# A quarter of the weight product moved from the front of a graph kernel into the first graph's chain

## The chip, the cores and the metric

The kernel runs on one core of a Trainium2 chip. The metric is the device time of one execution in microseconds (us). A kernel's time is the median over its runs. The profile is one profiled execution; its span is 1.7 to 1.9 us shorter than the device time of the same kind of run.

A ratio of two kernels is the mean time of one kernel's fast runs over the mean of the other's fast runs of the same rounds. It is therefore not quite the ratio of the medians that are quoted.

## The reference, cut to what matters

64 graphs, each with 256 nodes and 512 features, go through two layers. Layer 0 aggregates neighbours and multiplies by weights; layer 1 scores each node and weights its value by a softmax over the 256 nodes.

```python
# layer 0
deg = sum(adj, -1);  agg = adj @ x / max(deg, EPS)
x = layernorm(x + relu(concat([x, agg]) @ W.T))
# layer 1
q, k = split(x @ Wqk);  v = x @ Wv
w = inv_scale * mask * sum(q * (adj @ (k * mask)), -1)
x = layernorm(x + softmax(w, axis=nodes) * v)
```

The kernel uses that q·(adj·k) needs only the product of the two halves of Wqk, which it computes once at the front, as four chunks of 128 rows. Products of 2x2 blocks use seven multiplications in place of eight, so there are sums of blocks (the tiles s, sa, tv, t) to be made by VectorE and GpSimd.

## The kernel before: the parts that matter

The front multiplies the weights, then the graphs are pipelined: graph i's layer 0, graph i-1's aggregation for layer 1 together with graph i's, and graph i-2's layer 1.

```python
ps = [ps_mm.tile([P, F], F32, name="mm") for _ in range(NF)]          # four banks
for a in range(NA):
    for c in range(NF):
        nc.tensor.matmul(ps[c], wqk[:, a, c * P:(c + 1) * P], wqk[:, NA + a, :],
                         start=(a == 0), stop=(a == NA - 1))
for c in range(NF):
    nc.scalar.copy(w1[:, c, :], ps[c])
...
def weight_sums(w, name):                 # four 1024-wide subtractions on VectorE
    ...
    nc.vector.tensor_sub(t1, b12, b11)
    nc.vector.tensor_sub(t2, b22, t1)
    nc.vector.tensor_sub(b12, b22, b12)
    nc.vector.tensor_sub(t4, b21, t2)     # the only one that reads chunk 3
...
def layer0_a(g):
    ...
    product(u, s["S3"], w["T3"], start=False)
    nc.scalar.copy(y[:, 1, :], u)                       # stall 1 waits for this copy
    nc.vector.tensor_add(y[:, 1, :], p5, y[:, 1, :])
def layer0_b(g):
    ...
    product(u, s["A22"], w["T4"], start=False)          # T4's product, in the same bank u
    nc.scalar.copy(own[:, 1, :], u)
    product(p5, s["S4"], w["B22"], start=False)
    nc.vector.tensor_add(y[:, 0, :], p5, y[:, 0, :])    # stall 2: the aggregation needs y
```

The scheduler may reorder what is not held; `tc.issue_after(x)` holds instructions of x's engine behind x.

## Time and profile before

| | kernel before |
|---|---|
| time, median (first 3 runs) | 1983.97 us (1983.8 to 1984.79) |
| span of the profile | 1982.8 us |
| TensorE busy | 1959.8 us, 99% |
| VectorE / ScalarE / GpSimd busy | 79% / 33% / 21% |
| first weights land | 5.07 us |
| layer 0 of graph 0 starts | 20.37 us |
| graph 1's T4 product starts | 48.83 us |
| last product starts, and lasts | 1970.47 us, 3.37 us |

TensorE has next to no idle time from graph 2 to the last graph, so whatever moves the pipeline's start moves its end by the same amount. That is why the last four rows cut the span into stretches. I call them:

- **F**: first weight-product record to the start of layer 0 (before: 20.37 - 5.07 = 15.30 us);
- **M**: start of layer 0 to graph 1's T4 product (48.83 - 20.37 = 28.46 us);
- **S**: from there to the start of the last product (1921.64 us);
- **L**: duration of the last product (3.37 us).

One fp32 matmul of 512 columns is two records of 0.429 us each.

### The profile page before, as it was taken

The numbers are of one execution on the slowest core, as the hardware profiler recorded it, in microseconds if no ns is written. First come the engines' busy times: TensorE is split into PE (matmuls) and PEld (weight loads), VectorE is DVE, ScalarE is ACT, GpSimd is POOL, SyncE is SP. The second block draws the span as 40 slices with busy tenths as digits, with TensorE's granted clock in tenths as the row PEclk, the third lists the DMA queues.
The fourth block names the chain that finished last, engine by engine and source line by source line (L and its number), as shares of the span: only waits on it lengthen the run. The fifth ranks groups of instructions, "written<-read, shape, count | busy, mean of one in ns | idle before, by whom it ended". The sixth has DMA issues, their size and how long they took to land.

```text
span 1982.8 us, 19678 instructions
## 1 busy us (share of the span) xinstructions
PE 1959.8 (99%) x5424; PEld 1018.5 (51%) x5424; DVE 1566.7 (79%) x3220; ACT 650.0 (33%) x1545; POOL 419.4 (21%) x518
## 2 busy tenths in 40 slices
PE   8999999999999999999999999999999999999997
PEld 3554555555555545555555555455555555554553
DVE  5677877888788778778887887787788878877877
ACT  2323333333233333333332333333333323333332
POOL 3122221221221222212112212222122122122200
PEclk9999999999999999999999999999999999999999
DMA  6333333333333333333333333333333333333311
GB/s 223 88 83 82 98 93 86 96 90 91 97 80 101 93 82 97 93 87 96 82 100 97 79 102 93 81 96 94 88 96 89 92 97 80 102 93 82 83 45 46
DMA packets 390493, 182.09 MB, mean 92 GB/s; under 512 B 281456, under 2 KB 355056, under 8 KB 390384
## 3 DMA queue, kind: packets, MB, share of 16 engines
q1 hardware_dynamic: 390384, 180.84, 33.9%
q8 instruction: 44, 0.72, 0.2%
q14 instruction: 65, 0.53, 0.1%
HBM read 114.10 MB, written 33.62 MB: 74 GB/s over the span
## 4 chain that ended last, share of the span: by engine, by line
PE 98%; DVE 1%; DMA 0%; ACT 0%; issue 0%; DVEq 0%
PE mm L162 77%; PE mm L262 19%; PE mm L131 1%; DMA wqk<-wqk_t 0%; DMA adj<-adj_t 0%; DVE st L185 0%; ACT vals L303 0%; DVE own L296 0%; ACT vals L225 0%; DVE o L396 0%; DVE vals L236 0%; DVE own L223 0%; DVE t L141 0%; DVE t L140 0%; DVE w L142 0%
## 5 line engine op out<-in xcount | busy, mean ns | idle before, releaser
L162 PE MATMUL mm<-w,s 128*128 128x512 f32 x1024 | 481.5, 592 | 1.4 <-ACT v L339 0.7
L162 PE MATMUL mm<-t,s 128*128 128x512 f32 x1024 | 462.1, 594 | 0.0
L162 PEld LDWEIGHTS mm<-t,s 128*128 128x128 f32 x1024 | 194.8, 190 | 243.6 <-issue 228.8
L162 PEld LDWEIGHTS mm<-w,s 128*128 128x128 f32 x1024 | 194.2, 190 | 193.4 <-issue 155.0
L162 PE MATMUL mm<-w,xT 128*128 128x512 f32 x512 | 240.9, 592 | 0.0
L162 PE MATMUL mm<-w,x1T 128*128 128x512 f32 x512 | 240.8, 592 | 0.0
L204 POOL TENSOR_TENSOR sa<-adj 128x128 f32<-128x128 f32 x64 | 45.9, 717 | 759.9 <-PE mm L262 758.4
L152 POOL TENSOR_TENSOR s<-xT 128x256 f32<-128x256 f32 x64 | 47.0, 734 | 706.5 <-PE mm L162 687.3
L262 PE MATMUL mm<-tv,sa 128*128 128x256 f32 x768 | 187.3, 379 | 0.4 <-DVE tv L252 0.4
L262 PEld LDWEIGHTS mm<-tv,sa 128*128 128x128 f32 x768 | 145.7, 190 | 75.8 <-issue 48.2
L236 DVE TENSOR_TENSOR vals<-mm,vals 128x512 f32<-128x512 f32 x64 | 44.2, 691 | 142.9 <-PE mm L162 142.9
L188 ACT ACTIVATE rstd<-mv,eps 128x2 f32<-128x2 f32 x129 | 38.0, 296 | 345.1 <-DVE mv L186 345.0
L162 PEld LDWEIGHTS mm<-w,xT 128*128 128x128 f32 x512 | 97.3, 190 | 94.7 <-issue 91.4
L162 PEld LDWEIGHTS mm<-w,x1T 128*128 128x128 f32 x512 | 97.1, 190 | 93.8 <-issue 90.4
L339 ACT COPY v<-mm 128x512 f32<-128x512 f32 x63 | 36.9, 586 | 283.2 <-PE mm L162 283.2
L162 PE MATMUL mm<-t,xT 128*128 128x512 f32 x256 | 126.7, 617 | 2.8 <-ACT vals L225 2.8
L162 PE MATMUL mm<-t,x1T 128*128 128x512 f32 x256 | 125.3, 612 | 0.0
L294 DVE SCALAR_TENSOR_TENSOR own<-zr,rdeg,own 128x512 f32<-128x512 f32 x128 | 107.6, 841 | 22.0 <-ACT zr L284 21.9
L262 PE MATMUL mm<-vals,adj 128*128 128x256 f32 x512 | 121.3, 379 | 1.9 <-DVE vals L236 1.9
L262 PEld LDWEIGHTS mm<-vals,adj 128*128 128x128 f32 x512 | 97.1, 190 | 43.6 <-issue 16.9
L218 ACT COPY own<-mm 128x512 f32<-128x512 f32 x64 | 37.5, 586 | 227.4 <-PE mm L162 227.4
L328 DVE SCALAR_TENSOR_TENSOR q<-mm,zr 128x512 f32<-128x512 f32 x126 | 84.7, 672 | 32.4 <-PE mm L162 32.4
(101 smaller groups left out, 2732.6 us busy)
## 6 DMA issues: line engine op xcount, KB each, us to landing
xT<-x_t SPq DMA_DIRECT2D x64, 512.0 KB
x<-x SPq DMA_DIRECT2D x64, 512.0 KB
x1T<-sq SPq DMA_DIRECT2D x1008, 32.0 KB
out<-o SPq DMA_DIRECT2D x63, 512.0 KB
adj<-adj_t SPq DMA_DIRECT2D x64, 256.0 KB
rows<-adj SPq DMA_DIRECT2D x64, 256.0 KB
row<-d SPq DMA_DIRECT2D x62, 128.0 KB
d<-turned SPq DMA_DIRECT2D x248, 0.2 KB
```

The costliest lines, as they stand in the source:

```text
L131: nc.tensor.matmul(ps[c], wqk[:, a, c * P:(c + 1) * P], wqk[:, NA + a, :], start=(a == 0), stop=(a == NA - 1))
L152: eng.tensor_add(s1, a21, a22)
L162: queued[0] = nc.tensor.matmul(ps, a[:, c, :], b[:, c, :], start=start and c == 0, stop=(c == H - 1), skip_group_check=True).ins
L188: nc.scalar.activation(rstd[:, :n], mv[:, :n, 1], AF.Ln, bias=eps)
L204: nc.gpsimd.tensor_add(sa[:, 0], a21, a22)
L218: began = nc.scalar.copy(own[:, 0, :], u)
L236: nc.vector.tensor_add(y[:, 0, :], p5, y[:, 0, :])
L262: nc.tensor.matmul(ps[:, k * HF:(k + 1) * HF], sumsA[g - k][a], w[b][:, n, :], start=start and n == 0, stop=True, skip_group_check=True)
L294: nc.vector.scalar_tensor_tensor(own[:, t, :], z[:, t, :], rdeg[:, t:t + 1], own[:, t, :], op0=OP.mult, op1=OP.add)
L328: nc.vector.scalar_tensor_tensor(q, a, 1.0, agg[:, t, :], op0=OP.mult, op1=OP.mult, accum_out=to)
L339: nc.scalar.copy(v[:, 0, :], u)
```

## The change

The intent: TensorE stalls in graph 0's chain, where nothing else is there to run. A quarter of the weight product (chunk 3, four matmuls) is taken out of the front and put into two of these stalls, half in each.

```diff
+    def weight_product(chunks, pause=NA):
+        ps = [ps_mm.tile([P, F], F32, name="mm") for _ in chunks]
         for a in range(NA):
-            for c in range(NF):
-                nc.tensor.matmul(ps[c], wqk[:, a, c * P:(c + 1) * P], wqk[:, NA + a, :],
+            for k, c in enumerate(chunks):
+                nc.tensor.matmul(ps[k], wqk[:, a, c * P:(c + 1) * P], wqk[:, NA + a, :],
                                  start=(a == 0), stop=(a == NA - 1))
-        for c in range(NF):
-            nc.scalar.copy(w1[:, c, :], ps[c])
+            if a + 1 == pause:
+                yield
+        for k, c in enumerate(chunks):
+            nc.scalar.copy(w1[:, c, :], ps[k])
+        yield
+    step(weight_product((0, 1, 2)), 2)
 ...
+    rest = weight_product((3,), NA // 2)
 ...
             began, added = layer0_a(i)
+        if i == 0:
+            step(rest)
 ...
             layer0_b(i)
+        if i == 0:
+            step(rest)
```

The rest of the diff keeps the weights' tile alive longer. The softmax of the last graph and its singly stored tiles, which the title of the change also names, stand in both kernels alike. What the diff does not show: the scheduler, seeing other times, also moves two of the four sums of layer 1's weights on VectorE, from before to after the subtractions that the aggregation needs.

More of the change, by code (lines that the diff above doesn't have):

```diff
@@ L100, in resnorm_kernel @@
     w1 = const.tile([P, 2 * NF, F], F32, name="w1")
-    setup = tc.tile_pool(name="setup", bufs=1)
-    with setup as sp:
-        wqk = sp.tile([P, 2 * NA, F], F32, name="wqk")
-        for a in range(NA):
-            src = wqk_t.rearrange("(h a p) f -> a p h f", p=P, h=2)[a]
-            first(wqk.rearrange("p (h a) f -> a p h f", h=2)[a], src)
-        w0_of = w_t.rearrange("(k h p) o -> k p h o", p=P, h=H)
-        for k in (0, 2):
-            first(w0[:, k * H:(k + 1) * H, :], w0_of[k])
-        load_t(0, first)
-        for k in (3, 1):
-            first(w0[:, k * H:(k + 1) * H, :], w0_of[k])
-        load(0, first)
-        mask_sb = const.tile([P, NT, B], F32, name="mask_sb")
-        first(mask_sb, mask_t)
-        load_t(1, first)
-        load(1, first)
-        loaded = first(w1[:, NF:, :], wv.rearrange("(c p) o -> p c o", p=P))
-        ident = const.tile([P, P], F32, name="ident")
-        make_identity(nc, ident)
-        eps = const.tile([P, 1], F32, name="eps")
-        nc.vector.memset(eps, LN_EPS)
-        wide = [const.tile([P, Q], F32, name=f"wide{k}") for k in (0, 1)]
-        for w in wide:
-            nc.vector.memset(w, 0.0)
-        ps = [ps_mm.tile([P, F], F32, name="mm") for _ in range(NF)]
-        for a in range(NA):
-            for c in range(NF):
-                nc.tensor.matmul(ps[c], wqk[:, a, c * P:(c + 1) * P], wqk[:, NA + a, :],
-                                 start=(a == 0), stop=(a == NA - 1))
-        for c in range(NF):
-            nc.scalar.copy(w1[:, c, :], ps[c])
@@ L135, in resnorm_kernel @@
-    late = ctx.enter_context(tc.tile_pool(name="late", bufs=2))
+    setup = ExitStack()
+    wqk = setup.enter_context(tc.tile_pool(name="setup", bufs=1)).tile([P, 2 * NA, F], F32, name="wqk")
+    for a in range(NA):
+        src = wqk_t.rearrange("(h a p) f -> a p h f", p=P, h=2)[a]
+        first(wqk.rearrange("p (h a) f -> a p h f", h=2)[a], src)
+    w0_of = w_t.rearrange("(k h p) o -> k p h o", p=P, h=H)
+    for k in (0, 2):
+        first(w0[:, k * H:(k + 1) * H, :], w0_of[k])
+    load_t(0, first)
@@ new lines, in resnorm_kernel @@
+    for k in (3, 1):
+        first(w0[:, k * H:(k + 1) * H, :], w0_of[k])
+    load(0, first)
+    mask_sb = const.tile([P, NT, B], F32, name="mask_sb")
+    first(mask_sb, mask_t)
+    load_t(1, first)
+    load(1, first)
+    loaded = first(w1[:, NF:, :], wv.rearrange("(c p) o -> p c o", p=P))
+    ident = const.tile([P, P], F32, name="ident")
+    make_identity(nc, ident)
+    eps = const.tile([P, 1], F32, name="eps")
+    nc.vector.memset(eps, LN_EPS)
+    wide = [const.tile([P, Q], F32, name=f"wide{k}") for k in (0, 1)]
@@ new lines, in resnorm_kernel @@
+    for w in wide:
+        nc.vector.memset(w, 0.0)
+    def weight_product(chunks, pause=NA):
+        ps = [ps_mm.tile([P, F], F32, name="mm") for _ in chunks]
+        for a in range(NA):
+            for k, c in enumerate(chunks):
+                nc.tensor.matmul(ps[k], wqk[:, a, c * P:(c + 1) * P], wqk[:, NA + a, :],
+                                 start=(a == 0), stop=(a == NA - 1))
+            if a + 1 == pause:
[3 more added lines that the diff above has]
+        yield
@@ L137, in weight_sums, with step @@
+    def step(gen, n=1):
+        for _ in range(n):
+            next(gen, None)
+    step(weight_product((0, 1, 2)), 2)
     def weight_sums(w, name):
@@ L464, in resnorm_kernel @@
     prepare(0)
-    def step(gen, n=1):
-        for _ in range(n):
-            next(gen, None)
+    rest = weight_product((3,), NA // 2)
     for i in range(B + LAG - 2):
@@ L474, in resnorm_kernel @@
         if i == 1:
+            setup.close()
+            late = ctx.enter_context(tc.tile_pool(name="late", bufs=2))
             W1 = weight_sums(w1, "t1_")
```

## The prediction

> **What bounds the kernel now.** I read the page first: part 1 for the engine that is full, part 4 for the chain that ends last.
>
> ```profile
> PE 1959.8 (99%) x5424; PEld 1018.5 (51%) x5424; DVE 1566.7 (79%) x3220; ACT 650.0 (33%) x1545; POOL 419.4 (21%) x518
> PE 98%; DVE 1%; DMA 0%; ACT 0%; issue 0%; DVEq 0%
> ```
>
> TensorE is busy for 1959.8 of 1982.8 us and makes up 98% of the chain. So only a shorter TensorE list or fewer TensorE gaps can shorten the run. The diff keeps all 5424 matmul records; only gaps can be won. The view of busy time by stretches says where gaps are: from 75 to 1940 us TensorE is busy in 1865.00 of 1865.00 us. The gaps lie before 75 us and after 1940 us. The second place is not touched: the last graph's softmax and its tiles stored singly, which the change's title names, are already in the kernel before, and a listing of both kernels' instructions by engine shows no difference there.
>
> The beginning, TensorE alone (start, duration, then what it is; in brackets the idle time ahead of it and who ended it):
>
> ```profile
> 5.07 15.46 PE L131 MATMUL mm<-wqk 128*128 128x512 f32 x32 [5.07 <-DMA wqk<-wqk_t]
> 20.37 1.88 PE L162 MATMUL mm<-w,xT 128*128 128x512 f32 x4
> ...
> 27.23 1.88 PE L162 MATMUL mm<-w,s 128*128 128x512 f32 x4
> 29.79 1.98 PE L162 MATMUL mm<-t,xT 128*128 128x512 f32 x4 [0.68 <-ACT vals L225]
> 31.61 1.88 PE L162 MATMUL mm<-w,s 128*128 128x512 f32 x4
> 34.64 1.13 PE L262 MATMUL mm<-vals,adj 128*128 128x256 f32 x4 [1.15 <-DVE vals L236]
> 36.20 0.67 PE L262 MATMUL mm<-tv,sa 128*128 128x256 f32 x2 [0.43 <-DVE tv L252]
> ...
> 48.83 1.98 PE L162 MATMUL mm<-t,xT 128*128 128x512 f32 x4 [1.65 <-ACT vals L225]
> ```
>
> The reader is to see that 32 records (16 fp32 matmuls, two records each) multiply the weights, then graph 0 runs alone and stalls three times, because each product accumulates in a bank that ScalarE or VectorE must read first. Graph 1 stalls once more at 48.83. Later stalls (0.79 us at 53.31, 0.51 us at 70.61) depend on the same chain.
>
> VectorE in the same stretch, which ends two of the stalls:
>
> ```profile
> 29.77 0.69 DVE L226 TENSOR_TENSOR vals<-mm,vals 128x512 f32<-128x512 f32 x1 [1.30 <-ACT vals L225]
> 30.38 1.22 DVE L140 TENSOR_TENSOR t<-w 128x1024 f32<-128x1024 f32 x1
> 31.63 1.23 DVE L141 TENSOR_TENSOR t<-w,t 128x1024 f32<-128x1024 f32 x1
> 32.77 1.22 DVE L142 TENSOR_TENSOR w<-w 128x1024 f32<-128x1024 f32 x1
> 33.91 0.68 DVE L236 TENSOR_TENSOR vals<-mm,vals 128x512 f32<-128x512 f32 x1
> 34.51 1.21 DVE L143 TENSOR_TENSOR t<-w,t 128x1024 f32<-128x1024 f32 x1
> 35.64 0.42 DVE L252 TENSOR_TENSOR tv<-vals 128x256 f32<-128x256 f32 x1
> ...
> 39.95 0.42 DVE L281 TENSOR_TENSOR zr<-mm,zr 128x256 f32<-128x256 f32 x1 [1.82 <-ACT zr L280]
> 41.19 0.75 DVE L294 SCALAR_TENSOR_TENSOR own<-zr,rdeg,own 128x512 f32<-128x512 f32 x1 [0.81 <-ACT zr L284]
> ```
>
> The four sums of layer 1's weights (L140 to L143) sit between graph 0's own steps, and L143 delays L252.
>
> **What the Trainium skill says.** "Perfetto Trace Analysis", section "Optimizing Tensor Performance / Matmuls", says that independent matmul groups should rotate through PSUM banks so that one's evacuation overlaps the next one's matmuls. That is the change: chunk 3 of the weight product has a bank of its own. The trace agrees that the gaps are evacuations (ACT L225 0.59 us, DVE L236 0.68 us). "SBUF — State Buffer", section "Who interferes with whom", says that a VectorE instruction with two SBUF inputs contends with a GpSimd one that reads SBUF, and the second blocks. The trace agrees: a 1024-wide subtraction takes 1.22 us at 32.77, alone, but 1.75 us at 16.25 beside GpSimd. "TensorE: Matmul & The Clock Gate", section "What's actually happening", says the clock is halved until TensorE has been busy for a free-running window of about 3.4 us. The trace agrees: weight loads are 0.85 us apart up to 7.79 us, then 0.43 us.
>
> **The change, step by step.** A warm record of 512 columns starts 0.429 us after the one before (27.23 to 25.52 is 1.71 us for 4).
>
> 1. Removed at the front: 4 matmuls, 8 records, 8 x 0.429 = 3.43 us. Layer 0 starts at 20.37 - 3.43 = 16.94. The slow start costs the same. Are its inputs there? xT released GpSimd at 13.15, the T sums end at 12.9, 16.3, 18.0 and 19.4, and they are needed from 18.66, 20.37, 23.80 and 27.2 on. Yes.
> 2. Added at stall 1: S3's product runs 23.80 to 25.52; then 4 records of chunk 3 take 1.72 us, to 27.23. The copy L225 started 1.92 us after that product's start (29.15 - 27.23), so now 25.72, and ends at 26.3. The stall is gone: T4 starts at 27.23. Against before, 29.79 - 27.23 = 2.56 us earlier.
> 3. Added at stall 2: S4's product 28.95 to 30.66 (no exposed weight load after a wait, 0.1 us saved), then 4 records to 32.38. L236 can start 1.92 us after 28.95, at 30.87, and the new VectorE order puts it after L140 alone, so it ends at 31.56, hidden. The aggregation starts at 32.38, 2.26 us earlier than 34.64.
> 4. Stall 3: the new order has one sum (L141) instead of L143 ahead of L252, so L252 starts near 32.7. Before, TensorE followed 0.56 us after its start, so 33.2; the aggregation's first four records of 0.214 us end at 33.24. The stall just vanishes. 36.20 - 33.24 = 2.96 us earlier.
> 5. Moved cost: L142 and L143 now come after L255, ahead of L281. L281 would be wanted at 39.95 - 2.96 = 37.0. VectorE ends L255 near 35.1; two sums end at 37.5 alone, or near 38.2 if GpSimd's four sums of graph 2, which a DMA released at 36.04 before and should release near 33.3 now, lie beside them. L281 is thus 0.5 to 1.2 us late. It holds back one TensorE product, but graph 1's 1.65 us stall follows, so that is absorbed unless L287 and the normalisation behind it are late. They wait for that product: 38.6 + 0.1 + 0.43 + 0.2 = 39.3 against a wanted 38.9. So 0 to 0.4 us of the gain returns as a longer stall of graph 1.
> 6. ScalarE: the fourth copy (0.59 us) moves to about 32.6, inside an idle stretch of 2.98 us. No cost.
>
> Sum: 2.96 - (0 to 0.4) is about 2.65 us at graph 1's stall. After it the order is identical, and TensorE never waits from 75 to 1940 us, so the shift reaches the end whole. 1983.97 - 2.65 = 1981.3 us.
>
> **The rivals.**
> - *VectorE's chain takes over.* Its queue from 30 us to 48 us is already nearly solid (4.97 of 5 us busy from 30 to 35). If the displaced sums come fully late, with contention, L281 costs over 1 us more and the gain is only about 1.5 us: 1982.5. For it: step 5's margin is negative already. Against: the 0.81 us of idle time ahead of L294 and graph 1's stall take most of it up.
> - *A transfer at the front.* With three chunks instead of four per quarter, TensorE wants each quarter of wqk 0.9 to 2.6 us sooner, and DMA moves 407 GB/s from 5 to 10 us, its 16 engines full. If a quarter were late, the start would lose what it gained: 1983 to 1984. Against: VectorE got the first two pieces of w, issued after wqk, at 11.68. At that rate 0.52 MB lands every 1.3 us, so by an estimate quarter 4 lands near 9 us, wanted at 13.9.
> - *The clock at the tail.* The last product takes 3.37 us for 4 records at 1970.47, half speed, after 2.69 us without TensorE work. A shift changes where this stall falls in the free-running window. If it ran warm, 1.6 us more would be won: 1979.7. That would be chance, not the change; it may be what the 1 us spread of the runs before shows.
> - *No gain.* If each filled gap only moved the wait to the next link, the time would stay at 1984. Against: the fill is 3.43 us against 4.9 us of stalls and ramps before 36.20 and nothing else ran there.
>
> **Range and chances.** The central sum gives 1981.3. VectorE's contention can take about 1.2 us, the spread of the runs some 0.5 us: 1983.1 above. A warm tail or a fully absorbed step 5 gives 1979.8 below. 2% would be 40 us, and all the gaps before 75 us add to about 6 us beside the first load's 5.1 us, so faster by over 2% is nearly impossible. Slower by over 2% would need a broken steady state, where the order is unchanged.
>
> **What would show it.** Right: 24 records of the weight product at the front, ending near 16.9; records of it at 25.5 and 30.7; T4 at 27.2; the aggregation at 32.4; its second part at 33.2 without a wait; graph 1's T4 near 46.0 to 46.3 with a wait of 1.7 to 2 us; every later product about 2.65 us earlier. Wrong: a wait for wqk inside the first 24 records (front transfer), L142 or L143 of over 1.6 us with TensorE waiting for L281 and graph 1's T4 later than 46.8 (VectorE), or a last product of 1.9 us (tail clock). A gain under 1 us would make the prediction wrong.

## The result, and the profile after

| | before | after |
|---|---|---|
| median | 1983.97 us (1983.44 to 1984.79, 6 runs) | 1982.4 us (1981.6 to 1982.5, 6 runs) |
| span of the profile | 1982.8 us | 1980.7 us |
| F / M / S / L | 15.30 / 28.46 / 1921.64 / 3.37 us | 13.19 / 29.43 / 1921.68 / 3.02 us |

The ratio is 0.9991, with a 95% interval of 0.9978 to 1.0004: the interval holds 1, although the slowest of the six runs after (1982.5) is faster than the fastest of the six before (1983.44). How large the effect is, and where it comes from, is read from the trace, because the stretches can be read to some hundredths of a us.

The page's busy line and its chain, for the changed kernel:

```profile
PE 1960.3 (99%) x5424; PEld 1020.7 (52%) x5424; DVE 1569.6 (79%) x3220; ACT 648.5 (33%) x1545; POOL 414.6 (21%) x518
PE 98%; DVE 1%; ACT 0%; issue 0%; DMA 0%; DVEq 0%
```

The work is the same 5424 records, and TensorE is still the whole chain. Now TensorE alone in the timeline of the changed kernel (start, duration, what; in brackets the idle time ahead and who ended it):

```profile
4.42 13.36 PE L132 MATMUL mm<-wqk 128*128 128x512 f32 x24 [4.42 <-DMA wqk<-wqk_t]
17.61 1.88 PE L171 MATMUL mm<-w,xT 128*128 128x512 f32 x4
...
26.20 1.88 PE L132 MATMUL mm<-wqk 128*128 128x512 f32 x4
27.91 1.88 PE L171 MATMUL mm<-t,xT 128*128 128x512 f32 x4
...
31.35 1.88 PE L132 MATMUL mm<-wqk 128*128 128x512 f32 x4
33.06 1.03 PE L271 MATMUL mm<-vals,adj 128*128 128x256 f32 x4
33.93 0.60 PE L271 MATMUL mm<-tv,sa 128*128 128x256 f32 x2
...
38.98 0.70 PE L271 MATMUL mm<-vals,sa 128*128 128x256 f32 x2 [0.58 <-DVE zr L290]
...
47.04 1.98 PE L171 MATMUL mm<-t,xT 128*128 128x512 f32 x4 [1.36 <-ACT vals L234]
```

24 records stand at the front, four in each of the two stalls (26.20 and 31.35), and the brackets of the three stalls of graph 0 are gone. A new bracket has come at 38.98: TensorE waits 0.58 us for VectorE's L290 (L281 in the kernel before). And the front lasts 13.19 us, though 24 records at 0.429 us are 10.30.

VectorE of the changed kernel around the new wait (L151 and L152 are the two displaced sums):

```profile
33.29 0.42 DVE L261 TENSOR_TENSOR tv<-vals 128x256 f32<-128x256 f32 x1
...
35.17 1.75 DVE L151 TENSOR_TENSOR w<-w 128x1024 f32<-128x1024 f32 x1
36.84 1.75 DVE L152 TENSOR_TENSOR t<-w,t 128x1024 f32<-128x1024 f32 x1
38.51 0.41 DVE L290 TENSOR_TENSOR zr<-mm,zr 128x256 f32<-128x256 f32 x1
```

Both sums take 1.75 us where they took 1.22 us before, and L290 follows directly behind them. GpSimd was making graph 2's sums at that time:

```profile
35.80 1.71 POOL L162 TENSOR_TENSOR s<-s,xT 128x256 f32<-128x256 f32 x1
37.58 1.59 POOL L164 TENSOR_TENSOR s<-xT,s 128x256 f32<-128x256 f32 x1
```

**Where the 2.1 us of the span came from.** All from the starts quoted:

| stretch | gain, us | of which |
|---|---|---|
| first weights landed sooner | 0.65 | 5.07 - 4.42; not the change: 4.36 to 5.07 us in four traces with four chunks at the front |
| F | 2.11 | 3.43 for 8 records fewer, less 1.32 for a longer slow start |
| M | -0.97 | 3.43 put in, 2.46 of it into idle time |
| S | -0.04 | the shift goes through the pipeline whole |
| last product to the end | 0.35 | 12.33 - 11.98; L is 0.35 shorter |
| sum | 2.10 | 1982.8 - 1980.7 |

So the change itself is worth 3.43 - 0.97 = 2.46 us in this pair of traces. Two questions are open. Why does the change win 0.5 us less than the filled stalls did? (The second part of the aggregation, at 36.20 and 33.93 us, lies 15.83 and 16.32 us behind layer 0's start, so up to there 3.43 - 0.49 = 2.94 us were won.) And is the longer slow start the change's doing, or chance?

### The profile page after: what moved, and what is told of

Its sections match the earlier page's. It is cut to its first block, busy times and chain, and to the rows that moved or that the text cites. A ratio compares the mean times of both kernels' runs of the same rounds, so it can differ in the third digit from the quotient of the medians.

```text
span 1980.7 us, 19677 instructions
## 1 busy us (share of the span) xinstructions
PE 1960.3 (99%) x5424; PEld 1020.7 (52%) x5424; DVE 1569.6 (79%) x3220; ACT 648.5 (33%) x1545; POOL 414.6 (21%) x518
## 4 chain that ended last, share of the span: by engine, by line
PE 98%; DVE 1%; ACT 0%; issue 0%; DMA 0%; DVEq 0%
PE mm L171 78%; PE mm L271 19%; PE mm L132 1%; DMA wqk<-wqk_t 0%; ACT vals L312 0%; DVE st L194 0%; DVE t L152 0%; DVE w L151 0%; DVE o L405 0%; DVE vals L245 0%; DVE t L150 0%; DVE own L303 0%; DVE o L200 0%; DVE x L200 0%; DVE v L400 0%
## 5 line engine op out<-in xcount | busy, mean ns | idle before, releaser
L161 POOL TENSOR_TENSOR s<-xT 128x256 f32<-128x256 f32 x64 | 46.8, 731 | 703.6 <-PE mm L171 687.2
```

Of the source, the lines that this page charges most:

```text
L161: eng.tensor_add(s1, a21, a22)
```

## The experiments

My theory: each filled stall is worth what it was long; the two displaced sums, slowed by GpSimd, give 0.5 us back; and the slow start is TensorE's clock, by chance. The rivals: graph 1's stall is set by something else; what counts is only that the matmuls left the front; three chunks instead of four make the slow start longer; the slow start is the weights' transfer.

All twelve runs computed correct results. The stretches of every trace, in us ("slow" is F less 0.429 for each record, the cost of the half-speed start):

| kernel | time | F | slow | M | S | L |
|---|---|---|---|---|---|---|
| before | 1983.97 | 15.30 | 1.57 | 28.46 | 1921.64 | 3.37 |
| before_again | 1983.97 (1 run) | 15.48 | 1.75 | 28.46 | 1921.56 | 3.12 |
| before_third | 1984.95 (1 run) | 15.26 | 1.53 | 29.44 | 1921.77 | 3.14 |
| before_late_xt | 1983.89 | 16.61 | 2.88 | 28.47 | 1921.70 | 1.88 |
| after | 1982.40 | 13.19 | 2.89 | 29.43 | 1921.68 | 3.02 |
| again | 1982.48 | 13.18 | 2.88 | 29.42 | 1921.55 | 2.90 |
| again_b | 1982.45 (1 run) | 13.26 | 2.96 | 29.42 | 1921.71 | 2.99 |
| again_c | 1982.51 (1 run) | 12.71 | 2.41 | 29.42 | 1921.68 | 3.50 |
| late_xt | 1981.20 | 11.95 | 1.65 | 28.87 | 1921.72 | 3.51 |
| sums_late | 1980.87 | 13.20 | 2.90 | 28.87 | 1921.53 | 1.88 |
| one_stall | 1982.37 | 13.06 | 2.76 | 31.68 | 1921.48 | 1.88 |
| spread | 1979.64 | 12.54 | 2.24 | 28.09 | 1921.55 | 1.88 |
| warm_front | 1980.80 | 11.06 | 0.76 | 30.07 | 1921.56 | 1.88 |
| spread_warm | 1978.35 | 10.36 | 0.06 | 28.67 | (tail changed) | 1.88 |

### again: the changed kernel unaltered

> The changed kernel unaltered, as a control. Four stretches of TensorE's trace are read in every run: F from the first weight-product record to the start of layer 0, M from there to graph 1's T4 product, S from there to the last product, L the last product. Changed kernel so far: F 13.19, M 29.43, S 1921.68, L 3.02 us; before: 15.30, 28.46, 1921.64, 3.37. Theory (the filled stalls give 2.5 us, and the clock's slow start took 1.3 us of it back by chance): M and S repeat within 0.1 us, F comes out different by tenths up to 1.5 us because the number of half-speed records at the start is not fixed (11.9 us would mean a start as short as in the profile of before). Rival (the change itself prolongs the slow start): F is 13.2 again. Time 1982.4, within 0.7.

The five runs lie between 1980.52 and 1983.2 us (median 1982.48; before beside it 1984.03; ratio 0.999, 0.9977 to 1.0004). M is 29.42 and F 13.18. The control repeats M to 0.01 us. F did not move, so this run spoke for the rival; the question stayed open until before_late_xt. That one kernel on one chip scatters over 2.7 us says that end-to-end times alone cannot settle half a microsecond here.

### sums_late: the two displaced sums held back

The sums may be held behind given instructions; `paired[1]` is graph 1's first addition to vals.

```diff
-            W1 = weight_sums(w1, "t1_")
 ...
             began, added = layer0_a(i)
+        if i == 1:
+            W1 = weight_sums(w1, "t1_", (None, None, paired[1], paired[1]))
```

> Only VectorE's order is changed: the last two sums of layer 1's weights are held behind graph 1's addition to vals, so they no longer stand ahead of graph 0's zr addition. Theory of step 5 (they gave back 0.5 us): TensorE's wait of 0.6 us for that addition is gone, M is 29.43 - 0.48 = 28.95 us, and the time is 0.5 us below the control, 1981.9. Rival (graph 1's stall is set by ScalarE's chain and not by these sums): M stays 29.4, time the same.

M fell to 28.87, 0.55 us below the control, and the wait for the zr addition is gone:

```profile
38.19 0.60 PE L273 MATMUL mm<-vals,sa 128*128 128x256 f32 x2
```

The displaced sums are what gave the gain back; the rival is refuted. (Where they stand now, at 47 us, they also take 1.22 us each; the next run separates place and collision.) The time is 1980.87 us (1980.62 to 1981.15), more than the 0.5 us below the control. In the profiled pair 1.02 us of that is L, 1.88 us in place of 2.90, and 0.30 us earlier weights; the edit touches neither.

### late_xt and before_late_xt: the collision with GpSimd taken away

One transfer changes its place in the queue, so that GpSimd's four sums of graph 2 no longer fall beside VectorE's. No other instruction moves on any engine.

```diff
         dma(xs[g], x[g]...)
-        return load_t(g, dma)
+        if g == 2: return got             # graph 2's xT not yet
+        if g == 3: load_t(2, dma)         # but behind graph 3's x
+        return load_t(g, dma)
```

> The changed kernel with one transfer moved: graph 2's xT is issued after graph 3's x instead of before, so GpSimd's four sums of it start near 46 us instead of 34 us; every other instruction keeps its place. Theory (half of what the displaced sums give back is the collision with GpSimd: each took 1.75 us instead of 1.22): both sums take 1.22 us, the addition behind them comes 1.06 us sooner, TensorE's wait for it falls from 0.6 us to under 0.1 us, and M falls from 29.43 to 28.9 to 29.1 us. Rival (the sums are late because of their place alone): M stays at 29.3 to 29.4, with a wait of 0.3 us or more.

VectorE in that run (L156, L157 and L295 are the lines that were L151, L152 and L290):

```profile
33.58 1.22 DVE L156 TENSOR_TENSOR w<-w 128x1024 f32<-128x1024 f32 x1
34.71 1.22 DVE L157 TENSOR_TENSOR t<-w,t 128x1024 f32<-128x1024 f32 x1
36.22 0.42 DVE L295 TENSOR_TENSOR zr<-mm,zr 128x256 f32<-128x256 f32 x1 [0.28 <-ACT zr L294]
```

Both sums take 1.22 us, and the addition behind them waits for ScalarE again, as before the change: VectorE has time to spare. M is 28.87, exactly that of sums_late. So the expectation that the collision was only half of the loss was too small: without the collision the displaced sums cost nothing at all, and the whole 0.55 us is the collision. The time is 1981.2 us (1981.11 to 1981.35).

> The same transfer moved in the kernel before. There M was 28.46 us in two traces and 29.44 in a third, in which xT landed 0.5 us sooner after its issue and GpSimd's sums fell on VectorE's subtractions for the aggregation. Theory: with the collision gone M is 28.46 or less, by up to 0.5 us (the one subtraction that took 0.95 instead of 0.42), and the runs of before that lie near 1984.6 are missing: 1983.0 to 1983.9. Rival (the scatter of before is the clock alone): M 28.46 and the same scatter up to 1984.7.

M is 28.47, as in two of the three unaltered traces, and the four runs lie between 1983.6 and 1984.01 us, two of them just above the 1983.9 expected; of the nine runs of before beside them, five lie between 1984.5 and 1984.95. That fits the theory, but four runs and one trace with M as usual do not prove it, and the tail was fast in this trace (L 1.88).

With the transfer moved in both kernels, their two traces compare without the collision: M is 28.87 against 28.47, so the change is worth 3.43 - 0.40 = 3.03 us. That is the whole length of the three stalls (2.96 by the prediction's sum), with nothing given back.

Only one trace of before shows TensorE paying for the collision. It is the third, where it fell on other instructions than in the changed kernel, and it shows how it reaches TensorE. GpSimd, VectorE and TensorE of before_third:

```profile
35.07 0.72 POOL L152 TENSOR_TENSOR s<-xT 128x256 f32<-128x256 f32 x1 [6.05 <-DMA xT<-x_t]
```
```profile
35.12 0.95 DVE L252 TENSOR_TENSOR tv<-vals 128x256 f32<-128x256 f32 x1
36.00 0.94 DVE L254 TENSOR_TENSOR tv<-vals 128x256 f32<-128x256 f32 x1
```
```profile
36.23 0.67 PE L262 MATMUL mm<-tv,sa 128*128 128x256 f32 x2 [0.97 <-DVE tv L252]
```

xT landed 3.74 us after its issue at 31.33 here, and 4.20 us after it in the first trace (31.84 to 36.04). Half a microsecond of difference in a transfer put GpSimd's sums on VectorE's L252 and L254 (0.95 us in place of 0.42), and M became 29.44. The kernel before paid for the collision in one of three traces; the changed kernel paid in all four.

The second finding of before_late_xt is its F: 16.61 us, a slow start of 2.88 us, with four chunks at the front. So four chunks at the front can start as slowly as three, see below.

### one_stall: all four matmuls in the first stall

```diff
-    rest = weight_product((3,), NA // 2)
+    rest = weight_product((3,), NA)
```

The displaced sums are held where the changed kernel has them.

> All four matmuls of chunk 3 in stall 1 instead of two and two; VectorE's order as in the changed kernel. Theory (each fill is worth only what the stall there was long): stall 2 is back with about 1.3 us of waiting for vals, T4 of graph 0 is 1.72 us later than in the control relative to layer 0's start, M is about 31.0 us, and the time is 1.6 us above the control, about 1984.0, so the change's gain is lost. Rival (what counts is that they left the front, not where they went): M 29.4, time as the control.

TensorE of this run:

```profile
29.44 1.88 PE L173 MATMUL mm<-t,xT 128*128 128x512 f32 x4
...
33.82 1.13 PE L273 MATMUL mm<-vals,adj 128*128 128x256 f32 x4 [0.78 <-DVE vals L247]
...
41.04 0.70 PE L273 MATMUL mm<-vals,sa 128*128 128x256 f32 x2 [1.12 <-DVE zr L292]
```

The second stall is back, and T4 starts 12.02 us after layer 0 in place of 10.30. M is 31.68, 2.26 us above the control: 1.72 us from T4, and 0.54 us more of waiting for zr (1.12 us in place of 0.58). The second part is most of the 0.7 us by which it exceeds the expected 31.0: beside the two displaced sums (1.75 us each, as in the control) a third VectorE subtraction, L264, now met GpSimd too and took 0.95 us in place of 0.42. Where the matmuls go is what counts. But the time did not show it: 1982.37 us (1981.68 to 1983.23, 4 runs), as the control. In the traces the loss of 2.26 us in M stands against 0.96 us won from the last product's start to the end, 0.31 us of earlier weights, 0.12 us in F and 0.07 us in S, and the spans differ by only 0.8 us. The times of the two kernels overlap; this is a miss for the expected time and a hit for the mechanism.

### spread: the chunk fitted to the stalls

```diff
-    rest = weight_product((3,), NA // 2)
+    rest = weight_product((3,), (1, 2, NA))     # one matmul, one, two
 ...
+        if i == 1:
+            with tc.issue_after(queued[0]):
+                step(rest, 2)                   # in graph 1's stall
```

Of the sums of layer 1's weights one is held behind graph 0's first addition to vals, the others behind graph 1's first addition to vals and the end of its aggregation sums.

> Chunk 3 fitted to the stalls: one matmul (0.86 us) in stall 1, one in stall 2, two in graph 1's stall of 1.8 us; the sums of layer 1's weights later in VectorE's idle stretches. Theory: stall 1 costs 0.85 us less than in the control, the aggregation of graph 0 comes 1.6 us sooner, the 0.48 us of the sums are not given back, and the two matmuls in graph 1's stall are free: M about 27.3 us, time about 2.1 us below the control, 1980.3. Rival (VectorE's chain sets graph 1's T4 whatever TensorE does): M 28.5 to 29.4, gain under 1 us.

TensorE in graph 1's stall, and the stall of graph 0 that stayed:

```profile
33.25 0.67 PE L273 MATMUL mm<-tv,sa 128*128 128x256 f32 x2 [0.43 <-DVE tv L263]
...
44.07 1.88 PE L132 MATMUL mm<-wqk 128*128 128x512 f32 x4
45.88 1.99 PE L173 MATMUL mm<-t,xT 128*128 128x512 f32 x4
```

M is 28.09, 1.33 us below the control and less than before's 28.46, though four matmuls more lie in it. It is 0.8 us longer than the 27.3 expected. The wait of 0.43 us for tv stayed, because the first weight sum was issued ahead of that subtraction. And graph 1's T4 starts 3.53 us after the product ahead of it, as in before (45.30 to 48.83): its bank is free only after a ScalarE copy, at 45.26 here, which runs directly behind the masking of graph 0's x, and that waits for VectorE's normalisation. So the two matmuls in this stall cost nothing, but T4 would not come sooner without them: the rival was right in part. The time is 1979.64 us (1979.41 to 1980.8), ratio 0.9979 to before. That it is below the 1980.3 expected although M missed is luck: in the traces L was 1.02 and F 0.64 us shorter than the control's, and only the first weights were 0.58 us later.

### before_again, before_third, again_b, again_c, warm_front: the slow start

> The kernel before, unaltered, for a second trace of its beginning. So far F (first weight-product record to layer 0) was 15.30 us there, with half-speed records until 7.8 us, and 13.06 to 13.20 us (12.54 once) in five traces with three chunks at the front, with half-speed records until 8.8 to 10 us. Full speed throughout would be 32 x 0.429 = 13.73 us and 24 x 0.429 = 10.30 us. Theory (length of the half-speed start is chance): F here differs from 15.30, up to 16.7. Rival (three chunks make the slow start longer): F is 15.30 within 0.1 again. M is 28.46 in either case.

> The kernel before once more, a third sample of F, with the same two expectations: chance puts F anywhere from 15.0 to 16.7, the rival keeps it at 15.30. The last product lasts 1.9 us at full speed or up to 3.4 us at half; in before it was 3.37.

> The changed kernel a third time, for the half-speed start. Its first two traces have F 13.19 and 13.18, those of before 15.30, 15.48 and 15.26; at full speed these would be 10.30 and 13.73, so the start cost 2.9 us and 1.5 to 1.75. The first six records are the same in both kernels and already last different times, so the number of chunks cannot be the cause by itself. Theory (chance of the moment): one of the two further traces shows F below 12.5. Rival (each build has its own moment): F is 13.2 again.

> The changed kernel a fourth time, as again_b: chance puts F below 12.5 in at least one of the two; if each build has its own moment, F is 13.2 in both. M is 29.4 in both.

In the trace of after the weight loads show where full speed begins:

```profile
9.70 0.34 PEld L132 LDWEIGHTS mm<-wqk 128*128 128x128 f32 x1 [0.52 <-issue]
10.32 0.19 PEld L132 LDWEIGHTS mm<-wqk 128*128 128x128 f32 x1 [0.28 <-issue]
```

Taken alone, three traces of before with 1.53 to 1.75 us and four of the changed kernel with 2.41 to 2.96 us look like an effect of the change; again_c came down to F 12.71, not below 12.5, so my expectation failed. But before_late_xt, whose TensorE list is that of before, has 2.88 us, and late_xt, whose TensorE list is that of after, has 1.65 us. Both lengths occur with both lists. The first six records are the same work in all these kernels, too. So the number of chunks does not by itself set the slow start. Whether a build has a preferred moment, which the clustering suggests (without the warming matmuls, a slow start of over 2 us in seven of eight traces with three chunks, in one of four with four), stays open.

> The changed kernel with eight 128x128 matmuls of the identity ahead of the weight product, while TensorE would wait for the first quarter of the weights; their result is overwritten. Theory (the slow start is the clock and goes by TensorE's recent activity): F is 10.3 to 11.0 us instead of 13.2, layer 0 starts at 15.0 to 15.5 instead of 17.6, the time falls by about 2 us to 1980.4, and its spread shrinks. The scheduler reorders some instructions of graph 0 for this kernel, so M may differ by some tenths. Rival (the slow start is the transfers of the weights arriving): F plus the wait ahead of it stays, layer 0 starts at 17.6 again and the time is that of the changed kernel, 1982.4.

```diff
         ps = [ps_mm.tile([P, F], F32, name="mm") for _ in chunks]
+        if 0 in chunks:
+            for k in range(8):
+                nc.tensor.matmul(ps[0][:, :P], ident, ident, start=True, stop=True)
```

```profile
1.36 3.78 PE L132 MATMUL mm<-ident 128*128 128x128 f32 x16 [1.36 <-POOL ident masks.py:199]
5.12 11.22 PE L135 MATMUL mm<-wqk 128*128 128x512 f32 x24
16.18 1.88 PE L174 MATMUL mm<-w,xT 128*128 128x512 f32 x4
```

F is 11.06 us, and 10.36 in spread_warm, where the slow start is all but gone (0.06 us). Layer 0 starts at 16.18, later than the 15.0 to 15.5 expected, but the first weights came at 5.12 in place of the control's 4.67. So the slow start is TensorE's own speed, which follows its recent work, and not the transfer of weights: in spread_warm 24 records at full speed find all their weights there. About 0.6 us of M was lost again (30.07). The trace has two new waits of layer 0 (0.66 us at 20.44, 0.86 at 30.13) and puts both down to GpSimd's tile sa, which these products do not read. By the kernel they wait for their banks: the first for a copy that ScalarE now makes behind three copies of weight chunks, the second for an addition that VectorE now makes behind a weight sum:

```profile
18.32 1.53 ACT L140 COPY w<-mm 128x512 f32<-128x512 f32 x3
19.74 0.60 ACT L230 COPY own<-mm 128x512 f32<-128x512 f32 x1
29.36 0.66 DVE L238 TENSOR_TENSOR vals<-mm,vals 128x512 f32<-128x512 f32 x1
```

That is the scheduler's new order, and no run here undoes it. The time is 1980.8 us (1979.79 to 1981.79), 0.4 above the expected, and the spread did not shrink as expected: 2.0 us.

### spread_warm: a version faster than both

```diff
+        product(p5, s["S1"], w["T1"])           # ahead of the last score transposes
         with tc.issue_after(queued[0]):
             e = softmax_rows(g)
 ...
-        product(p5, s["S1"], w["T1"])
```

This on top of spread and the eight warming matmuls.

> The spread kernel with the same eight matmuls at the front, and the last graph's product of S1 and T1 moved ahead of the score transposes, into the 2.7 us in which TensorE waits for the scores. Theory: 2 us from the front, 1 to 2.5 us from the tail against spread's 1979.6, so 1976 to 1977. Rival (the tail is set by VectorE's chain, and the moved product only shifts the wait): 1977.6 or more.

1978.35 us (1978.18 to 1978.53), ratio 0.9972 (0.9959 to 0.9984) to before: 5.5 us below the 1983.89 of before beside it, and with the smallest scatter of the changed kernels but late_xt. It is above the 1976 to 1977 expected and above the rival's bound of 1977.6. The product did move and ran at full speed, but VectorE then ended the tail: TensorE waited 2.09 us for the scores and 1.66 us for the softmax behind them. Layer 0 also waited 1.10 us for a late ScalarE copy, as in warm_front (M 28.67 against spread's 28.09).

### The tail's two speeds

The last product runs right after TensorE has waited 2.69 us (2.70 in some traces) for the scores. After, and then sums_late:

```profile
1968.72 3.02 PE L171 MATMUL mm<-t,s 128*128 128x512 f32 x4
```
```profile
1967.97 1.88 PE L173 MATMUL mm<-t,s 128*128 128x512 f32 x4
```

The same four records took 2.90 to 3.51 us in eight of thirteen traces and 1.88 us in five, all with the tail's instructions unchanged. That is up to 1.6 us of the end-to-end time. What decides between the two speeds no run here shows; the kernel before has both (3.12 to 3.37 us in three traces, 1.88 in before_late_xt).

## Why the prediction came out as it did

The time lay inside the range, 1.1 us above the predicted 1981.3; the gain was 1.6 us by the medians in place of 2.65. The mechanism was right: three stalls filled, and a part given back at graph 1. Luck helped the number in the profiled pair: 1.32 us more of slow start, which the prediction had ruled out, stand against 0.65 us of earlier weights and 0.35 us of a faster tail, which are not the change's either.

- **Step 1** (8 records, 3.43 us off the front) held in size. Its sentence "The slow start costs the same" failed: it cost 2.89 us in place of 1.57. That is the term that was mis-sized most, by 1.32 us. before_late_xt and late_xt show that both lengths occur with either list.
- **Steps 2 to 4** held to 0.02 us when counted from layer 0's start. Predicted and measured: T4 at 10.29 and 10.30, aggregation at 15.44 and 15.45, its second part at 16.30 and 16.32 us. All three stalls vanished.
- **Step 5** had the right place, order and cause, and named the collision with GpSimd. L290 came 20.90 us after layer 0's start in place of the wanted 20.06, 0.84 us late and inside the 0.5 to 1.2 us. What comes back as a longer stall of graph 1 was to be 0 to 0.4 us; the traces show 0.5 (15.83 + 12.63 before, 16.32 + 13.11 after), and sums_late and late_xt win back 0.55. That the sums would make it 0.5 us late even "alone", without GpSimd, was wrong: in late_xt the addition comes 19.99 us after layer 0's start, which is not late, and nothing is lost.
- **Step 6** (ScalarE's moved copy costs nothing) held: no wait of TensorE names it.
- **The sum** at graph 1's stall was to be 2.65; the change's own part is 2.46, and S (1921.48 to 1921.77 us in thirteen traces) shows that it reaches the end whole.
- **The rivals.** VectorE's chain took its 0.5 us; by my own sign ("L142 or L143 of over 1.6 us with TensorE waiting for L281 and graph 1's T4 later than 46.8") it was met, at 47.04, but 0.67 us of that is layer 0's later start. The transfer at the front did not bind: warm_front ran 24 records faster than either kernel. The tail's clock did not run at full speed: 3.02 us in place of 3.37 in the profile, worth 0.35. Later traces have both speeds in kernels with the same tail. "No gain" is refuted by M, and the fill could never have won its whole 3.43 us against stalls of 2.96.
- **What I had not foreseen**: that the kernel before has a second M of its own, 29.44 us. Against such a run the change is worth the full 3.43 us.
- **Small sums that do not come out**, without effect on the result: quarter 4 would be wanted at 16.94 - 6 x 0.429 = 14.4 us, not 13.9; the stalls and the slow start before 36.20 us add to 2.96 + 1.57 = 4.5 us, not 4.9; TensorE's idle time before 75 us is 10.27 - 5.07 = 5.2 us, not 6.

## What to carry to other kernels

Independent work put into a stall is worth the length of that stall and no more; count it from the last common point of the two traces, because fills of 0.4 us can be read there and not in end-to-end times that scatter by 2 us. Look at what the scheduler moves besides: two VectorE sums that slid beside GpSimd's work took back 0.5 of 3 us, and moving one transfer brought it back. When a trace names an engine for a wait, check in the kernel that the waiting instruction reads or overwrites what that engine made: two waits of warm_front are put down to the wrong one. Where TensorE waits at the front anyway, a few discarded matmuls bring it up to speed before the real ones.

## What the Trainium skill lacked or had wrong

- "TensorE: Matmul & The Clock Gate", "What's actually happening": the slow start is there, with a window of about 3.4 us and the warning that it varies by run. Here the first weight load at full speed came 3.2 us to 6.0 us after the first record (5.07 to 8.35 us in before, 4.42 to 10.32 us in after), which cost 1.5 to 3.0 us. That is a wider range than the page's plus or minus 500 ns, and the page does not say that one kernel may show 5.0 to 6.0 us in trace after trace.
- The same section has the clock halved after an idle window of about 3.4 us. Here a shorter wait, of 2.69 us, was followed by a product wholly or partly at half speed in eight of thirteen traces (2.90 to 3.51 us in place of 1.88).
- The same page, under "Seeing it yourself", warns that the trace's clock events are unreliable, but not in which direction. Here the profile's granted clock read full while records ran at half speed: it was 1.00 from 4.4 to 10.0 us in the trace of after, with weight loads 0.85 us apart; in the slow tail it read 0.59.
- "SBUF — State Buffer", "Who interferes with whom": right as to who collides, and the numbers here put a price on it. A 1024-wide subtraction took 1.75 us in place of 1.22, a 256-wide one 0.95 in place of 0.42, and GpSimd's own sums up to 1.71 in place of 0.72. The page speaks of the one that starts second; here both sides became slower in turn, and both of two VectorE sums in a row were delayed.
